# Twelve-layer decoder on one core: the second attention's rotation and its clears go from GpSimd to VectorE

## The chip, the cores and the metric

The kernel runs on one core of one Trainium2 chip. The core has TensorE for matrix products (PE, with its weight loads PEld shown apart), VectorE (DVE), ScalarE (ACT), GpSimd (POOL) and SyncE (SP), which issues the transfers. The metric is the device time of one execution in microseconds (us), lower is better. A profiled execution gives, besides its own time, a trace of every instruction. TensorE's clock is granted by the chip and is seen in the trace as a share of full speed: 1.00, or 0.50.

## The reference

A post-norm decoder of four levels with three sublayers each, on x of shape 4 x 256 x 256 (1024 rows, handled as 8 tiles of 128) and a context of 4 x 256 x 128:

```python
x = layernorm(x + L0_attn(x));  x = layernorm(x + L0_ssm(ctx, x));  x = layernorm(x + L0_ffn(x))
x = layernorm(x + L1_attn(x));  x = layernorm(x + L1_ssm(ctx, x));  x = layernorm(x + L1_ffn(x))
...
```

The second attention, L1, is what is changed. It has 16 query heads and 4 key heads of 16 columns, and a rotation of neighbouring column pairs before the scores:

```python
x0, x1 = xp[..., 0], xp[..., 1]
r0 = x0 * cos - x1 * sin
r1 = x0 * sin + x1 * cos
...
weights = softmax(Qr @ Kr.T / 4);  out = (weights @ V) @ W_o
```

The L1 state-space layer (`ssm`) depends on the context alone until its last gate, so the kernel runs its scan beside other layers. The L0 feed-forward layer, here called the thought layer, makes four small refinement steps on the last row of each batch and gates the result into all rows.

## The kernel before

`decoder` runs the parts of a list one after the other (first attention, thought, second attention, experts and so on); x (128 rows x 8 tiles x 256) and its transpose xT stay in SBUF. The order in which each engine's instructions stand is fixed when the program is built: a planner merges what the code emits, so an instruction can stand well ahead of its place in the code once its memory is free. Each engine then works through its own queue in order and waits at an instruction until its inputs are there.

Three helpers matter: `K.tt` is a tensor-tensor operation on VectorE (profile line L111), `K.ptt` the same on GpSimd (L123), `K.mm` a product on TensorE (L132). `K.copy` alternates between VectorE (L98) and ScalarE (L100). `norm` (L153) takes the moments on VectorE (L160, L161), makes rstd in two GpSimd instructions (`root`: L169 and a power, L123) and scales x on VectorE (L117); then `turn_pair` (L182) transposes x on TensorE (L187).

The second attention is `run_gqa` (L982). It takes five tiles and clears parts of them: `kn` (keys as rows, L994 and L995), `qn` (queries as rows, L996), and `vt` (values, L997 and L998), besides `ones` (L999 to L1001). The head slots are 32 columns wide, and 16 of them are padding that must be zero, or one in the keys' maximum column. These clears stand on GpSimd between the end of the first attention and the start of the thought layer, at 378 to 384 us.

Then, for each of the 8 tiles: the products with the query, key and value weights go to one PSUM bank (`ps`, three banks), VectorE makes four products with cosine and sine into t0 to t3 (L1016 to L1019), the differences and sums of these go into `qn` (16 heads) and `kn` (4 heads) (L1020 to L1022), two copies put the values into `vt`, and the transposes of the tile before follow (`small_heads_T`, L787). Between the tiles stand the first steps of the row maxima (`heads16.begin`: score products `sc`, and reduces on VectorE, L129) and, per tile, one step of the scan (`K.scans.beside(1)`): two exponentials on ScalarE, and on VectorE a product with B, the scan (L520) and a product with C, later summed on TensorE into `ssmps`. After the eight tiles `heads16.run` goes on with scores, exponentials and sums, one scan step to each.

In the thought layer the names that the prediction uses are `w_d` (the weights whose mean is taken out), `centre`, `mean` and `cb` (set up on VectorE, L637 to L671), the gates of the 8 tiles (`gate`, L679, then one sigmoid), `xb` and `gx` (on GpSimd), and the scan's preparation: taps on the context, `u`, `xd`, `delta`, `du` (L451 to L487).

Of the kernel before, what the change touches and what calls it, by code (L numbers as in the profile page):

```python
# [29 lines left out]
ADD, SUB, MUL, MAX, MIN = ALU.add, ALU.subtract, ALU.mult, ALU.max, ALU.min  # L30
# [503 lines left out]
def gate_pair(K, pool, y, b):  # L534

    K.scans.upto(b)
    gate = pool.tile([P, DC, L], F32, name="gate")

    K.act(gate, K.x[:, 2 * b : 2 * b + 2, :], AF.Silu)
    K.ptt(gate, gate, y[:, :, b * L : (b + 1) * L], MUL)  # L540
    for t in range(2):
        ps = K.tp.tile([P, 512], F32, name="ps", tag="tp")
        for c in range(DC):
            K.nc.tensor.transpose(ps[:, c * P : (c + 1) * P], gate[:, c, t * P : (t + 1) * P], K.ident)
        K.add_out(2 * b + t, ps[:, 0:D])
# [236 lines left out]
def small_heads_T(K, dst, src, col, chunks, scales=None, tp=None):  # L782


    ps = (tp or K.tp).tile([P, 4, P], F32, name="ps", tag="tp")
    for c in range(chunks):
        K.nc.tensor.transpose(ps[:, c, :], src[:, c * P : (c + 1) * P], K.ident)  # L787
    if scales is None:
        K.copy(dst[:, :, col : col + P], ps[:, 0:chunks, :])
    else:  # L790
        for lo, hi, g, b in scales:
            K.copy_scaled(dst[:, :, col + lo : col + hi], ps[:, 0:chunks, lo:hi], g, b)
# [189 lines left out]
def run_gqa(K, w, more):  # L982
    nc, tc = K.nc, K.tc
    more()
    with ExitStack() as ctx:
        one = ctx.enter_context(tc.tile_pool(name="gqa1", bufs=1))
        wk = ctx.enter_context(tc.tile_pool(name="gqa2", bufs=2))
        qT = one.tile([P, 4, B * L], F32, name="qT")
        kT = one.tile([P, 1, B * L], F32, name="kT")
        qn = one.tile([P, NT, 16, 32], F32, name="qn")  # L990
        kn = one.tile([P, NT, 4, 32], F32, name="kn")
        vt = one.tile([P, NT, 4, 2, 32], F32, name="vt")
        ones = one.tile([P, 2, 32], F32, name="ones")
        nc.gpsimd.memset(kn[:, :, :, 16:32], 0.0)  # L994
        nc.gpsimd.memset(kn[:, :, :, 16:17], 1.0)  # L995
        nc.gpsimd.memset(qn[:, :, :, 16:32], 0.0)  # L996
        nc.gpsimd.memset(vt[:, :, :, 0, 16:32], 0.0)  # L997
        nc.gpsimd.memset(vt[:, :, :, 1, 0:16], 0.0)  # L998
        nc.gpsimd.memset(ones, 0.0)  # L999
        for j in range(2):  # L1000
            nc.gpsimd.memset(ones[:, j, 16 * j : 16 * j + 16], 1.0)  # L1001
        ctx.enter_context(K.turns(1))
        if K.first == 3 and K.fused(3):
            K.scans.begin("l1x")
        heads16 = SmallHeads(K, ctx, "gqa", qn, qT, kT, vt, ones, w["o"], [(0, L)])
        early = ctx.enter_context(ExitStack())
        pm = early.enter_context(tc.tile_pool(name="gqap", bufs=3, space=PSUM))
        for i in range(NT):
            ps = pm.tile([P, 512], F32, name="ps")
            for c in range(DC):  # L1010
                K.mm(ps[:, 0:384], K.xT[:, c, i * P : (i + 1) * P], w["qkv"][:, c, :], c == 0, c == DC - 1)
            pair = ps[:, 0:320].rearrange("p (h j two) -> p h j two", j=8, two=2)
            x0, x1 = pair[:, :, :, 0], pair[:, :, :, 1]
            cos, sin = (w["rope"][:, k, i % 2, :].rearrange("p (h j) -> p h j", j=8) for k in range(2))
            t = [wk.tile([P, 20, 8], F32, name=f"t{k}") for k in range(4)]
            K.tt(t[0], x0, cos, MUL)  # L1016
            K.tt(t[1], x1, sin, MUL)
            K.tt(t[2], x0, sin, MUL)
            K.tt(t[3], x1, cos, MUL)  # L1019
            for dst, hs in ((qn, slice(0, 16)), (kn, slice(16, 20))):  # L1020
                K.ptt(dst[:, i, :, 0:8], t[0][:, hs], t[1][:, hs], SUB)
                K.ptt(dst[:, i, :, 8:16], t[2][:, hs], t[3][:, hs], ADD)  # L1022
            for j in range(2):
                K.copy(vt[:, i, :, j, 16 * j : 16 * j + 16], ps[:, 320:384].rearrange("p (h d) -> p h d", d=16))
            for k in ([i - 1] if i else []) + ([i] if i == NT - 1 else []):
                small_heads_T(K, qT, qn[:, k].rearrange("p h s -> p (h s)"), k * P, 4)
                small_heads_T(K, kT, kn[:, k].rearrange("p h s -> p (h s)"), k * P, 1)

            heads16.begin((0, 0, 1, 1, 1, 1, 2, 2)[i])
            K.scans.beside(1)  # L1030
        early.close()
        if K.fused(3):
            heads16.then = lambda b: gate_pair(K, wk, K.scans.y, b)
        heads16.run(ctx, lambda: K.scans.beside(1))
# [1183 lines left out]
def load_none(K, wp):  # L2218
# [5 lines left out]
    (load_none, run_gate("l0x")),  # L2224
    (load_thought, run_thought),
    (load_gqa, run_gqa),
    (load_none, run_gate("l1x")),
    (load_moe, run_moe),
# [209 lines left out]
```

## Time and profile before

| what | us |
|---|---|
| median of three runs (lowest, highest) | 2461.45 (2458.55, 2464.18) |
| the profiled execution | 2461.66 |
| its span on the engines | 2459.9 |
| mean granted TensorE clock | 0.947 |
| busy: TensorE, VectorE, ScalarE, GpSimd | 2267.6, 1464.3, 801.9, 288.5 |
| the clears of the second attention, on GpSimd | 378.7 to 384.1 |
| the thought layer, about | 374 to 526 |
| the rotation of the second attention, first to last product with the weights | 527.7 to 562.0 |
| rest of the second attention and of the scan, about | 562 to 756 |

The span starts with the first instruction and ends with the last; the execution is some 1.8 us longer than it. Busy time of a stage is no measure of what it costs: an engine that is filled may still be waited for by nobody. What a change is worth is read where the wait ends last: a line of the view in time shows an instruction's start and duration, and in brackets how long its engine stood idle before it and whose result ended the wait.

### The profile page before, as it was taken

How to read it: one execution, taken by the hardware profiler on the slowest of the kernel's cores; microseconds unless marked ns; L12 is line 12 of the kernel's file. 1: busy time of each engine (PE TensorE's matmuls, PEld its weight loads, DVE VectorE, ACT ScalarE, POOL GpSimd, SP SyncE). 2: the span in 40 equal slices, each digit the busy share in tenths (PEclk: the TensorE clock that was granted, in tenths of full speed). 3: DMA queues.
4: the chain of work that ended last, by engine and by line, in shares of the span. 5: the costliest groups of instructions: out<-in, count | busy, mean ns of one | idle time of the engine just before them, and what ended most of it. 6: DMA issues, size and time to landing. Idle time of an engine off the chain costs nothing. (4 is left out here: it accounts for less than half of the span.)

```text
span 2459.9 us, 28697 instructions
## 1 busy us (share of the span) xinstructions
PE 2267.6 (92%) x10620; PEld 1520.1 (62%) x10624; DVE 1464.3 (60%) x2986; ACT 801.9 (33%) x1781; POOL 288.5 (12%) x455
## 2 busy tenths in 40 slices
PE   8899997769996999899999999999999988899997
PEld 4566763335433555536888888888776543476774
DVE  4799982888985211280455544445556677774566
ACT  3577664513441111162211111111022244343434
POOL 0000014130010322200011000110210002100001
PEclk9999997767887999999999999999998899999999
DMA  6222221312213544220222112110100002100000
GB/s 201 61 60 60 53 61 27 80 41 48 52 39 101 164 131 127 81 78 9 73 82 87 46 46 73 47 63 31 46 22 1 20 18 71 41 1 1 1 1 18
DMA packets 132835, 138.99 MB, mean 57 GB/s; under 512 B 13876, under 2 KB 120726, under 8 KB 130904
## 3 DMA queue, kind: packets, MB, share of 16 engines
q1 hardware_dynamic: 132696, 137.16, 19.5%
q8 instruction: 84, 1.38, 0.2%
q14 instruction: 55, 0.45, 0.1%
HBM read 134.27 MB, written 2.85 MB: 56 GB/s over the span
## 5 line engine op out<-in xcount | busy, mean ns | idle before, releaser
L132 PE MATMUL ps<-xw,xcT 128*128 128x256 f32 (+1 forms) x2304 | 518.9, 382 | 0.3 <-ACT YT L126 0.3
L132 PEld LDWEIGHTS ps<-xw,xcT 128*128 128x128 f32 x2304 | 430.8, 190 | 64.0 <-issue 1.9
L132 PE MATMUL sc<-kT,qT 32*128 32x256 f32 (+2 forms) x1024 | 239.2, 404 | 9.6 <-DVE qn L129 9.2
L132 PEld LDWEIGHTS sc<-kT,qT 128*128 128x128 f32 (+1 forms) x1024 | 152.6, 200 | 86.0 <-issue 52.4
L111 DVE TENSOR_TENSOR xp<-ps,xb 128x256 f32<-128x256 f32 x96 | 40.4, 421 | 230.7 <-PE ps L132 230.6
L126 ACT ACTIVATE dA<-delta,negA 128x255 f32<-128x255 f32 x256 | 118.2, 501 | 142.0 <-DVE s L520 139.1
L132 PE MATMUL ssmps<-s,idz 128*128 128x512 f32 x256 | 146.7, 678 | 18.9 <-DVE s L111 18.0
L520 DVE TENSOR_TENSOR_SCAN s<-dA,s 128x512 f32<-128x512 f32 x128 | 155.0, 1218 | 2.6
L126 ACT ACTIVATE p<-sc,nm 128x256 f32<-128x256 f32 (+1 forms) x256 | 112.0, 444 | 96.5 <-DVE nm L129 90.5
L111 DVE TENSOR_TENSOR hT<-u,a 128x512 f32<-128x512 f32 x48 | 33.1, 690 | 184.0 <-PE u L132 184.0
L126 ACT ACTIVATE sq<-xp 128x1024 f32<-128x1024 f32 x24 | 25.4, 1057 | 314.1 <-DVE xp L111 314.1
L132 PE MATMUL o<-pT,vt 128*128 128x256 f32 (+1 forms) x352 | 116.2, 452 | 12.3 <-ACT pT L332 11.9
L169 POOL TENSOR_SCALAR rstd<-mv 128x2 f32<-128x2 f32 x48 | 11.8, 245 | 887.5 <-DVE mv L161 877.7
L129 DVE TENSOR_REDUCE qn<-sc 128x2 f32<-128x480 f32 (+1 forms) x192 | 87.0, 505 | 37.9 <-PE sc L132 36.4
L126 ACT ACTIVATE e<-sT 128x512 f32<-128x512 f32 x128 | 70.9, 591 | 108.4 <-PE sT L132 108.2
L132 PE MATMUL sT<-q,kT 32*128 32x256 f32 (+1 forms) x384 | 102.3, 508 | 3.5 <-ACT e L126 3.3
L1474 DVE TENSOR_TENSOR_SCAN dec<-xT,idz 128x256 f32<-128x256 f32 (+1 forms) x192 | 89.7, 535 | 21.5 <-DMA xT<-ad 21.5
L129 DVE TENSOR_REDUCE nm<-sc 128x2 f32<-128x512 f32 (+1 forms) x128 | 77.3, 612 | 41.2 <-PE sc L132 40.7
L126 ACT ACTIVATE a<-g 128x512 f32<-128x512 f32 x48 | 28.7, 598 | 206.2 <-PE g L132 203.4
L111 DVE TENSOR_TENSOR s<-du,bc 128x512 f32<-128x512 f32 x128 | 87.7, 691 | 11.0 <-POOL du L123 7.7
L123 POOL TENSOR_TENSOR xp<-xp,rn 128x128 f32<-128x128 f32 x96 | 35.2, 403 | 476.9 <-DVE rn L1406 476.9
L132 PE MATMUL g<-xT,wj 128*128 128x512 f32 x192 | 90.3, 593 | 0.7 <-ACT rows L100 0.7
(503 smaller groups left out, 4027.2 us busy)
## 6 DMA issues: line engine op xcount, KB each, us to landing
bc<-bcd SPq DMA_DIRECT2D x128, 256.0 KB, 4.6
xw<-in_l2a_xw_dram SPq DMA_DIRECT2D x24, 768.0 KB, 4.8
xT<-ad SPq DMA_DIRECT2D x12, 1024.0 KB, 4.3
wj<-in_l1f_gate_dram SPq DMA_DIRECT2D x48, 128.0 KB, 2.7
wj<-in_l1f_up_dram SPq DMA_DIRECT2D x48, 128.0 KB, 2.9
wj<-in_l1f_down_dram SPq DMA_DIRECT2D x48, 128.0 KB, 3.1
sel<-cwd SPq DMA_DIRECT2D x32, 192.0 KB, 3.2
sel<-cwd SPq DMA_DIRECT2D x32, 128.0 KB, 3.5
```

The lines of the kernel that those rows point to most:

```text
L111: self.nc.vector.tensor_tensor(out=out, in0=a, in1=b, op=op)
L123: self.nc.gpsimd.tensor_tensor(out=out, in0=a, in1=b, op=op)
L126: self.nc.scalar.activation(out, in_, func, **kw)
L129: self.nc.vector.tensor_reduce(out=out, in_=in_, axis=AX.X, op=op, **kw)
L132: self.nc.tensor.matmul(out, lhsT=lhsT, rhs=rhs, start=start, stop=stop)
L169: self.nc.gpsimd.tensor_scalar(out=out, in0=in_, scalar1=add, scalar2=None, op0=ADD)
L520: nc.vector.tensor_tensor_scan(out=s.rearrange("p c l -> p (c l)"), data0=dA.rearrange("p c l -> p (c l)"), data1=s.rearrange("p c l -> p ...
L1474: nc.vector.tensor_tensor_scan(out=dec[:, k, h, :], data0=ap[:, h, at(bb, k, j) : at(bb, k, 2)], data1=K.idz[:, 0 : (2 - j) * P], initial=0.0,
```

## The change

The five clears of `kn`, `qn` and `vt` are issued on VectorE; the clears of `ones` stay on GpSimd. In the rotation the four differences and sums of each tile are issued on VectorE; for the eight tiles these are 32 instructions.

```diff
-        nc.gpsimd.memset(kn[:, :, :, 16:32], 0.0)
-        nc.gpsimd.memset(kn[:, :, :, 16:17], 1.0)
-        nc.gpsimd.memset(qn[:, :, :, 16:32], 0.0)
-        nc.gpsimd.memset(vt[:, :, :, 0, 16:32], 0.0)
-        nc.gpsimd.memset(vt[:, :, :, 1, 0:16], 0.0)
+        nc.vector.memset(kn[:, :, :, 16:32], 0.0)
+        nc.vector.memset(kn[:, :, :, 16:17], 1.0)
+        nc.vector.memset(qn[:, :, :, 16:32], 0.0)
+        nc.vector.memset(vt[:, :, :, 0, 16:32], 0.0)
+        nc.vector.memset(vt[:, :, :, 1, 0:16], 0.0)
         nc.gpsimd.memset(ones, 0.0)
...
             for dst, hs in ((qn, slice(0, 16)), (kn, slice(16, 20))):
-                K.ptt(dst[:, i, :, 0:8], t[0][:, hs], t[1][:, hs], SUB)
-                K.ptt(dst[:, i, :, 8:16], t[2][:, hs], t[3][:, hs], ADD)
+                K.tt(dst[:, i, :, 0:8], t[0][:, hs], t[1][:, hs], SUB)
+                K.tt(dst[:, i, :, 8:16], t[2][:, hs], t[3][:, hs], ADD)
```

With the change the planner places the clears on VectorE behind x, the weight column, `centre` and `mean` of the thought layer's set-up, around `cb` and the first gate eviction. The new differences and sums stand directly behind the four products of their tile; in one tile two row maxima stand between them. Transfers are issued in the same order as before. Some instructions near both places change their order on TensorE and ScalarE: a sigmoid and an absolute value of the scan's preparation, and a few score products and products with the weights in the rotation.

## The prediction

> **What bounds the kernel now.** Part 1 of the page first, for the whole span:
>
> ```profile
> PE 2267.6 (92%) x10620; PEld 1520.1 (62%) x10624; DVE 1464.3 (60%) x2986; ACT 801.9 (33%) x1781; POOL 288.5 (12%) x455
> ```
>
> TensorE is the long engine and GpSimd the idle one, but that is an average over twelve layers. The chain of what ended last cannot help here: its list of pieces reaches back to 1780 us only, and the change acts at 378 to 384 us (the clears) and 530 to 570 us (the rotation). So I read those two places in the view in order of time, and the stretches around them in the table by stretches.
>
> The clears, in order of time, one engine after the other (start, duration, engine, line, what, and in brackets the idle time before it):
>
> ```profile
> 375.97 2.81 POOL L123 TENSOR_TENSOR xb<-x,r_l0f_rows 128x256 f32<-128x256 f32 x4
> 378.73 0.51 POOL L994 MEMSET kn<- 128x512 f32 x1
> 379.19 1.79 POOL L996 MEMSET qn<- 128x2048 f32 x1
> 380.97 0.21 POOL L169 TENSOR_SCALAR rstd<-mv 128x2 f32<-128x2 f32 x1
> 381.12 0.14 POOL L995 MEMSET kn<- 128x32 f32 x1
> 381.19 0.51 POOL L997 MEMSET vt<- 128x512 f32 x1
> 381.67 0.70 POOL L123 TENSOR_TENSOR rstd<-rstd,power 128x2 f32<-128x2 f32 x1
> ...
> 382.41 1.00 DVE L117 TENSOR_SCALAR x<-x,mv,rstd 128x256 f32<-128x256 f32 x2 [4.28 <-POOL rstd L123]
> ...
> 383.24 1.13 PE L187 MATMUL ps<-idz,x 128*128 128x128 f32 x4 [4.22 <-DVE x L117]
> ```
>
> The reader is to see a queue on GpSimd that costs time: the variance was ready at 377.18, the two instructions that make rstd of it stand behind and between four clears, VectorE waits 4.28 us for rstd and TensorE 4.22 us for VectorE. Nothing else runs on TensorE then.
>
> The stretches (busy us with counts for PE, PEld, DVE, ACT, POOL; then the granted clock, the DMA share, GB/s):
>
> ```profile
> 379.00:383.00 4.00, 0.01 (x1) 0.00 (x0) 0.59 (x1) 0.00 (x0) 3.94 (x8) 0.78 0.00 0
> 383.00:392.00 9.00, 8.76 (x26) 5.05 (x27) 1.34 (x5) 5.66 (x12) 1.61 (x4) 0.53 0.00 0
> 530.00:545.00 15.00, 14.23 (x61) 8.10 (x60) 13.26 (x34) 3.83 (x13) 6.52 (x16) 0.95 0.20 50
> 545.00:552.00 7.00, 7.00 (x13) 3.46 (x13) 4.15 (x12) 0.40 (x2) 1.28 (x4) 0.51 0.15 37
> 552.00:569.00 17.00, 16.02 (x71) 8.57 (x70) 15.30 (x32) 4.55 (x13) 4.97 (x12) 1.00 0.15 32
> 569.00:600.00 31.00, 31.00 (x116) 17.42 (x117) 25.83 (x39) 9.84 (x20) 0.16 (x1) 0.51 0.22 49
> 600.00:645.00 45.00, 43.51 (x318) 21.41 (x318) 40.71 (x59) 19.91 (x41) 0.93 (x2) 1.00 0.30 58
> ```
>
> In the rotation two limits alternate. At full clock VectorE is filled (13.26 of 15 us, 15.30 of 17), and TensorE follows it. At half clock (545 to 552, 569 to 600) TensorE is filled and VectorE waits. GpSimd limits nothing there. Its two groups in 527 to 580 us, and where TensorE last waited before the long slow stretch:
>
> ```profile
> L123 POOL TENSOR_TENSOR qn<-t,t 128x128 f32<-128x128 f32 x16 | 9.8, 611 | 30.9 <-DVE t L111 30.9
> L123 POOL TENSOR_TENSOR kn<-t,t 128x32 f32<-128x32 f32 x16 | 4.0, 250 | 0.0
> ...
> 568.01 1.16 PE L132 MATMUL ssmps<-s,idz 128*128 128x512 f32 x2 [0.84 <-DVE s L111]
> ```
>
> GpSimd waits 30.9 us for VectorE. In the other direction the waits in 527 to 580 us hold 1.8 us of weight loads waiting for its qn and kn, in three waits.
>
> **The clears, taken off GpSimd.** Five clears go (514, 1794, 142, 514, 514 ns). In the built order GpSimd now has, behind the four xb, the three clears of `ones` (rows 0.14 and 0.15 for two) and then the two of rstd. The xb end at 378.78; 0.2 for the small clears puts the first at 379.0. The second starts 0.44 later where nothing stands between them (519.73 to 520.17 in the thought's end), takes 0.70 and ends at 380.1. VectorE's x starts 0.04 behind it (382.37 to 382.41), so at 380.15 for 382.41: 2.3 us sooner, and the transposes on TensorE with it (0.83 behind x, as now). Bounds: 2.2 to 2.4.
>
> **The clears, put on VectorE.** In the built order they stand behind x, the weight column, `centre` and `mean`; ScalarE waits for `mean` (7.62 us now), so that must not get late: 380.15 + 1.00 + 0.45 + 0.24 + 0.79 = 382.6, for 384.12 now. The trace has no clear on VectorE. From above: its reduce over the same 2048 elements takes 2.25 us. From below: GpSimd's own rows, 1.79. The Trainium skill (VectorE: DVE Perf Modes, Zero memsets can be issued as uint32) says a clear takes one cycle per element; at that page's 0.96 GHz 2048 elements are an estimated 2.13 us. I take 2.2, 0.6 for each of the three of 512 and 0.15: 4.2 us (3.5 to 4.5). They lie in VectorE's idle time, 2.98 us before `cb` (L671) and 6.47 us before the first gate eviction at 393.79. Queued behind them are `cb`, not read before `cs` at 417.8, and the gate evictions, which TensorE feeds later than the clears end. Cost nothing; without that cover up to 4.2.
>
> Sum of this place: -2.3 us. It is carried on, because TensorE has no gap from 383.24 to 404 and everything behind (conv taps, u, xd, delta) is released by it. The new order also sets one absolute value behind the sigmoid on ScalarE, and the token's turn ahead of the second x_proj product on TensorE; each moves a step by a microsecond or two, in both directions, and I set that at 0, bounds -1 to +1.5.
>
> **The rotation, put on VectorE.** Per tile of 128 rows two instructions of 128 elements and two of 32, eight tiles. The nearest VectorE rows are its four products of 160 elements: 312 ns each, but the four take 1.01 together, so a pitch of 0.235, that is 0.167 for the elements and 0.07 fixed. That makes 0.20 for 128 elements and 0.10 for 32; the sum that reads t3 straight behind its product waits for it another 0.1. Per tile 2 x 0.20 + 2 x 0.10 + 0.1 = 0.7, for eight 5.6 us (0.6 and 4.8 without that wait; 0.9 and 7 if every duration counts in full). Off GpSimd go 13.8 us that nobody but the transposes waited for.
>
> How much of 5.6 reaches the end? Behind the new instructions in VectorE's queue stand the vt copy, the eviction of qT, the scan step and the row maxima, and TensorE waits for these: the score banks are freed by the maxima. From 534.1 to 548.8 VectorE is busy without a gap, and tiles 0 to 4 fall before its end: tile 0 costs 0.5 (it waited 0.53 for TensorE behind it), 1 to 3 cost 0.7 each before TensorE's release at 545. But the tail behind tile 4 is hidden in the 2.85 us that VectorE waits for TensorE at 551.66. There tile 5 is 1.9 late. Tile 5 adds 0.7, and what tile 6 adds goes into the wait of 1.34 before the eviction at 563.43, whose chain on TensorE starts before it: 2.6 late. Tile 7 adds 0.7. So 3.3 us arrive at 570, and from there TensorE at half clock carries it unshortened. Bounds: 1.5 (the later qn no longer wait for GpSimd's 1.6 us per tile) to 5.6.
>
> A shared port is removed, too: one GpSimd qn took 1371 ns, against a median of 457, beside a scan of 1.31 for 1.22. Worth 0.1 to 0.3 on VectorE; inside the bounds.
>
> **The clock.** The trace: TensorE's clock halved at 381.6, 2.6 us after its last product; but also at 545.4 and 569.0, where it had just waited 0.47 and 0.84 us, with 0.6 and 0.9 us of idle time in the three us before. The Trainium skill (TensorE: Matmul & The Clock Gate, HAM oscillation) asks only that no gap pass some 3.4 us. By that rule added VectorE work, which makes gaps of 0.7 us, costs no clock, and the sum is -2.3 + 3.3 = +1.0. By this case's rows gaps of that size are what starts a slow stretch, so the rule does not hold here, and the measurement decides. TensorE will now wait up to 0.7 us more per tile where it waits on VectorE. The short slow stretch, 545.4 to 551.5, holds 6.1 us that are 3.05 us at full clock. I charge one more of these in 552 to 569, and that the long one starts with the score products at 566.03 and not at 569.0, 3 us at half clock, of which 1.5 are lost: together 4.5. Bounds: 0, and 8.5 if all of 552 to 569 runs at half clock.
>
> **Sum.** -2.3 + 3.3 + 4.5 = +5.5 us. The profiled execution took 2461.66 (span 2459.9 and 1.8 around it) and would take 2467.2; that execution is 0.2 above the median of 2461.45, so the median goes to 2467.0. 0.2%, 4.9 us, is about what a measurement of this kernel can tell from no change (its three runs span 0.23%).
>
> **Rivals.**
> *The work moves, the clock doesn't.* Slow stretches as now: +1.0, 2462.5 (-1.5 to +4). For it: the first drop follows TensorE's own waits for ScalarE, not VectorE. Against: 552 to 569 is at full clock with only 1 us of TensorE idle.
>
> *Faster, by the clock at the clears.* TensorE's gap at 379 shrinks from 4.2 to 1.9 us, below the 2.6 after which the clock fell. If it then stays up, 383.2 to 391.6 loses half of its 8.4 us: -4.2 more, -6.5 with the 2.3. This decides if the rotation then costs under 1.6 us, which it does if the later tiles' transposes come early enough to feed the slow stretch, or that stretch of 31 us ends sooner: VectorE has 5.2 us idle in it, all there is to win. With 0.5 for the rotation: -6.0, 2455.5. For it: the gap is arithmetic from rows. Against: gaps under a microsecond also brought the clock down.
>
> *Hidden anyway.* Rotation and clears both cost and bring nothing. The 4.22 us that TensorE waited for the clears speak against it; it lands at 2461.5 and is counted with the first rival.
>
> **How the numbers follow.** Forecast 0.42 (0.36 slower by over 0.2%, 0.06 within; its own range 2464 to 2475). First rival with "hidden" 0.28 (0.25 within, 0.03 slower). Clock at the clears 0.30 (0.24 faster, 0.05 within, 0.01 slower). That makes faster 0.24, within 0.36, slower 0.40. The range takes in the forecast up to +15 (5.6 arriving and 8.5 of clock, with 1.5 of order) and the faster case down to -8: 2453 to 2476.
>
> **What would show it.** x (L117) at about 380.2 and TensorE's gap there near 1.9 us; the granted clock of 383 to 392 above 0.9 would speak for the faster rival. Clears on VectorE of 2.1 to 2.3 us for qn. Thirty-two small products on VectorE, 0.7 us a tile. The end of the rotation about 1 us later against the start of the thought layer's gates if the clock stays; a stretch at 0.5 within 552 to 569 if I am right. I am wrong if the last rotation tile comes no later behind the first than now (37.4 us).

## The result: slower, and not where the sum put it

The changed kernel takes 2474.61 us (median of five runs, 2470.99 to 2478.76) against 2462.17 us of the kernel before (2458.55 to 2473.50, five runs); the ratio is 1.0044 [1.0027, 1.0061], that is 6.6 to 15 us more. The forecast of 2467.0 named the right sign, and the time lies in its range, but the two terms that made the sign, the rotation and the clock, are not what costs.

The profiled execution took 2478.76 us, the slowest of the five, with a span of 2477.0. It arrives at the clears 1.8 us later than the profiled execution before (first `xb` at 376.08 for 374.28), although nothing ahead of them differs. So stages are compared below by their own lengths, and totals by medians.

First the whole span, part 1 of the page of the changed kernel:

```profile
PE 2272.5 (92%) x10624; PEld 1525.6 (62%) x10624; DVE 1483.1 (60%) x3023; ACT 801.7 (32%) x1781; POOL 271.7 (11%) x418
```

VectorE's busy time rose by 18.8 us and GpSimd's fell by 16.8. The rotation's sums (6.2 busy, shown below) and the clears (3.3) explain 9.5 of VectorE's 18.8; the other 9.3 are more than covered by one waiting instruction, which counts as busy and is 10.6 us longer than before.

The clears, in order of time, in the changed kernel:

```profile
380.51 0.17 POOL L999 MEMSET ones<- 128x64 f32 x1
380.73 0.16 POOL L1001 MEMSET ones<- 128x16 f32 x2
380.86 0.22 POOL L169 TENSOR_SCALAR rstd<-mv 128x2 f32<-128x2 f32 x1
381.16 0.71 POOL L123 TENSOR_TENSOR rstd<-rstd,power 128x2 f32<-128x2 f32 x1
381.90 0.74 DVE L117 TENSOR_SCALAR x<-x,mv,rstd 128x256 f32<-128x256 f32 x2 [2.34 <-POOL rstd L123]
...
382.46 0.78 PE L187 MATMUL ps<-idz,x 128*128 128x128 f32 x4 [1.64 <-DVE x L117]
384.06 0.48 DVE L994 MEMSET kn<- 128x512 f32 x1
384.68 2.05 PE L132 MATMUL ps<-w_l0f_gate,xT 128*128 128x256 f32 x4
384.92 1.76 DVE L996 MEMSET qn<- 128x2048 f32 x1 [0.37 <-issue]
387.17 0.09 DVE L995 MEMSET kn<- 128x32 f32 x1
387.29 0.48 DVE L997 MEMSET vt<- 128x512 f32 x1
387.83 0.48 DVE L998 MEMSET vt<- 128x512 f32 x1
```

This place does what was forecast. VectorE waits 2.34 us for rstd instead of 4.28, TensorE 1.64 for 4.22. The clears take 3.3 us on VectorE and end at 388.3. One gate eviction stands among them (386.77); the next comes only when TensorE feeds it (391.75), and TensorE waits for none of this.

Now the place where the time goes. This is the token's turn in the thought layer of the changed kernel, in order of time:

```profile
401.08 1.91 ACT L126 ACTIVATE gate<-gate 128x2048 f32<-128x2048 f32 x1
401.17 0.38 PE L684 MATMUL last<-idz,xT 128*4 128x128 f32 x2
402.90 0.67 ACT L126 ACTIVATE du<-ssmps,w_l1x_cols 128x512 f32<-128x512 f32 x1
403.08 0.22 POOL L169 TENSOR_SCALAR trstd<-tmv 4x1 f32<-4x1 f32 x1 [19.10 <-DVE tmv L604]
403.38 0.56 POOL L123 TENSOR_TENSOR trstd<-trstd,power 4x1 f32<-4x1 f32 x1
403.92 1.39 POOL L123 TENSOR_TENSOR gx<-gate,r_l0f_rows 128x256 f32<-128x256 f32 x2
403.98 11.00 DVE L117 TENSOR_SCALAR r<-tok,tmv,trstd 4x256 f32<-4x256 f32 x1 [0.99 <-POOL trstd L123]
...
413.44 1.39 POOL L123 TENSOR_TENSOR gx<-gx,x 128x256 f32<-128x256 f32 x2
415.02 0.86 DVE L111 TENSOR_TENSOR r<-r,r_l0f_rows 4x256 f32<-4x256 f32 x2
415.93 0.37 PE L612 MATMUL ps<-idz,r 4*128 4x4 f32 x2 [14.39 <-DVE r L111]
416.24 3.64 PE L132 MATMUL ssmps<-u,w_l1x_xp 128*40 128x512 f32 x4
419.80 1.87 PE L132 MATMUL ps<-rT,w_l0f_agg 128*128 128x4 f32 x8
```

And the same steps in the kernel before:

```profile
406.78 0.40 DVE L117 TENSOR_SCALAR r<-tok,tmv,trstd 4x256 f32<-4x256 f32 x1 [0.99 <-POOL trstd L123]
407.21 0.86 DVE L111 TENSOR_TENSOR r<-r,r_l0f_rows 4x256 f32<-4x256 f32 x2
408.51 1.41 POOL L123 TENSOR_TENSOR gx<-gate,r_l0f_rows 128x256 f32<-128x256 f32 x2 [1.77 <-ACT gate L126]
```

One VectorE instruction on 4 x 256 elements, the scaling of the token, takes 11.00 us instead of 0.40. It starts 0.06 us after GpSimd has begun its sixteen `gx` instructions, and ends 0.15 us after the last of them. TensorE stands still for 14.39 us behind it. Before, `gx` waited for the sigmoid (1.77 us) and came only when `r` was done. In the changed kernel the sigmoid stands ahead of the second absolute value on ScalarE (401.08, then 402.90), so the gates are ready before the token is, and `gx` starts first.

The gap costs more than its length. Behind it TensorE ran at half clock: the granted clock of 415 to 424 us was 0.50. In the kernel with the clears alone (below), which has the same order and the same gap here, it was 0.71 in 413 to 420, and from `last` to the first square it took 20.6 us for 22.7.

Last the rotation of the changed kernel, in the table by stretches (the columns as in the prediction), from the first products with the weights on:

```profile
536.00:552.00 16.00, 15.05 (x53) 8.73 (x54) 14.79 (x46) 4.27 (x12) 0.00 (x0) 0.83 0.14 37
552.00:564.00 12.00, 11.76 (x51) 6.70 (x50) 12.00 (x30) 2.77 (x8) 0.00 (x0) 1.00 0.20 41
564.00:572.00 8.00, 5.90 (x21) 2.51 (x19) 8.00 (x24) 1.74 (x6) 0.00 (x0) 0.81 0.26 49
572.00:582.00 10.00, 9.83 (x29) 5.48 (x30) 8.43 (x20) 1.82 (x5) 0.00 (x0) 0.50 0.14 32
582.00:612.00 30.00, 30.00 (x125) 16.51 (x123) 24.03 (x35) 10.08 (x21) 0.00 (x0) 0.59 0.22 50
612.00:657.00 45.00, 43.09 (x317) 21.32 (x315) 42.24 (x61) 21.29 (x42) 1.95 (x3) 1.00 0.27 57
```

VectorE is filled (12.00 of 12 us, 8.00 of 8), as forecast. But no slow stretch was added: the stretch at full clock reaches from 552 to about 568, and the long slow one follows it for some 40 us (0.50, then 0.59), where before a short one (545 to 552) and a long one (569 to 600) stood. Over 75 us that begin some 9 us behind the first product with the weights the mean granted clock is the same, 0.75 (537 to 612 us before, 547 to 622 changed), and TensorE is busy for 72.96 and 72.49 us of them. The sums of the rotation on VectorE, among the groups of 537 to 590 us:

```profile
L111 DVE TENSOR_TENSOR qn<-t,t 128x128 f32<-128x128 f32 x16 | 3.9, 286 | 0.0
L111 DVE TENSOR_TENSOR kn<-t,t 128x32 f32<-128x32 f32 x16 | 2.3, 188 | 0.0
```

From the first pair of `qn` (542.05) to that of `kn` (542.45) and the copy behind it (542.66) it is 0.61 us a tile, 4.9 for eight; 5.6 was the estimate. From the first of these sums to the last of the eight tiles it is 37.6 us, before 37.4.

### The profile page after: what moved, and what is told of

It is laid out like the page before. It is cut to its first block, busy times and chain, and to the rows that moved or that the text cites. A ratio compares the mean times of both kernels' runs of the same rounds, so it can differ in the third digit from the quotient of the medians.

```text
span 2477.0 us, 28684 instructions
## 1 busy us (share of the span) xinstructions
PE 2272.5 (92%) x10624; PEld 1525.6 (62%) x10624; DVE 1483.1 (60%) x3023; ACT 801.7 (32%) x1781; POOL 271.7 (11%) x418
## 5 line engine op out<-in xcount | busy, mean ns | idle before, releaser
L132 PEld LDWEIGHTS ps<-xw,xcT 128*128 128x128 f32 x2304 | 430.8, 190 | 64.0 <-issue 1.9
L132 PE MATMUL sc<-kT,qT 32*128 32x256 f32 (+2 forms) x1024 | 242.1, 408 | 10.0 <-DVE qn L129 9.7
L132 PE MATMUL ssmps<-s,idz 128*128 128x512 f32 x256 | 145.9, 676 | 19.6 <-DVE s L111 18.8
L132 PE MATMUL u<-xT,wj 128*128 128x512 f32 x192 | 90.9, 595 | 0.0
```

Source lines behind the costliest of these rows:

```text
L132: self.nc.tensor.matmul(out, lhsT=lhsT, rhs=rhs, start=start, stop=stop)
```

## The experiments

The two theories. A: the loss comes from one collision. A VectorE instruction that needs an access to SBUF which, by this theory, it shares with GpSimd is held up while GpSimd's `gx` run back to back, and only the order brought about by the early clears lets the two meet. B is the prediction's: the clears gain, the added VectorE work in the rotation and the clock lose.

To compare profiles I measured each stage in the trace, in us, between marks that all kernels have: the first `xb` (376.08 above), the transposes into `last` (L684 above), the first square of the refinement steps (`sq`), the copy `lastmean` at their end, the first product with the weights of the second attention, its last `kn`, and the first copy of the experts' gates (`cwT`). Kernels that leave work out are not in the table.

| kernel | xb to last | to sq | to lastmean | to weights | to last kn | to cwT | sum |
|---|---|---|---|---|---|---|---|
| before | 29.9 | 6.9 | 67.8 | 48.8 | 41.2 | 242.9 | 437.5 |
| changed | 25.1 | 22.7 | 65.4 | 48.8 | 41.6 | 243.8 | 447.4 |
| clears alone | 25.1 | 20.6 | 64.9 | 48.8 | 40.7 | 242.5 | 442.7 |
| rotation alone | 29.0 | 6.9 | 67.0 | 48.8 | 41.7 | 242.4 | 435.9 |
| changed, token in PSUM | 25.1 | 8.5 | 66.8 | 48.8 | 42.3 | 242.2 | 433.7 |
| changed, scaling reads PSUM | 23.4 | 21.9 | 63.0 | 48.8 | 41.6 | 243.8 | 442.5 |
| changed, gx behind th | 25.1 | 10.1 | 68.0 | 48.8 | 42.5 | 244.4 | 439.0 |
| changed, token and th from PSUM | 26.7 | 12.4 | 63.3 | 48.8 | 41.6 | 243.7 | 436.5 |
| before, token in PSUM | 29.9 | 7.1 | 67.7 | 48.8 | 41.1 | 243.0 | 437.5 |
| changed, gx in pairs of tiles | 26.8 | 21.6 | 65.3 | 48.8 | 42.2 | 242.1 | 446.8 |
| changed, gx in halves | 25.1 | 12.6 | 68.4 | 48.8 | 41.7 | 243.9 | 440.5 |
| clears alone, token and th from PSUM | 23.4 | 8.1 | 67.0 | 48.8 | 40.9 | 242.7 | 430.8 |

The row of the kernel before and its control (fourth from below) differ by 0.2 us at most in any stage. Kernels with the same order still differ with the clock: the first column is 23.4, 25.1 and 26.7 us in three kernels with the clears on VectorE (scaling reads PSUM, changed, token and `th` from PSUM), at a mean granted clock of 1.00, 0.93 and 0.87. And behind the experts, where all kernels have the same code, the profiled executions took between 1648 and 1664 us. So a row says where time went in one execution; whether a kernel is faster is read from the medians.

### Each half of the change alone

The clears alone (the rotation stays on GpSimd, the clears as in the changed kernel):

```diff
-                K.tt(dst[:, i, :, 0:8], t[0][:, hs], t[1][:, hs], SUB)
-                K.tt(dst[:, i, :, 8:16], t[2][:, hs], t[3][:, hs], ADD)
+                K.ptt(dst[:, i, :, 0:8], t[0][:, hs], t[1][:, hs], SUB)
+                K.ptt(dst[:, i, :, 8:16], t[2][:, hs], t[3][:, hs], ADD)
```

> The five clears on VectorE, the rotation left on GpSimd. In the thought layer this kernel has the order of the changed kernel on every engine. Theory A (the port): there the sigmoid now stands ahead of the second absolute value, so GpSimd's 16 gx instructions start just before VectorE scales the last token's row (r, 4x256), and that instruction, 0.40 us before, lasts as long as they do, 11 us; expected r at 10 to 11 us and 2469 to 2473, nearly the whole loss. Theory B (the prediction's: VectorE's load in the rotation and the clock): the clears alone gain 2.3, 2459.

Measured: 2471.48 us (2468.63 to 2483.07), ratio to the kernel before 1.0037 [1.0021, 1.0054]. The scaling lasts 11.006 us, from 402.10, with `gx` from 402.05.

The rotation alone (the clears go back to GpSimd, the rotation stays on VectorE):

```diff
-        nc.vector.memset(kn[:, :, :, 16:32], 0.0)
...
+        nc.gpsimd.memset(kn[:, :, :, 16:32], 0.0)
```

> The rotation's differences and sums on VectorE, the clears left on GpSimd; the thought layer's order is that of the kernel before. Theory A: r stays at 0.40 us, and the rotation costs between nothing and 3 us: 2460 to 2465. Theory B: 3.3 of VectorE's time and 4.5 of clock, 2469.

Measured: 2464.41 us (2459.62 to 2470.35), ratio 0.9997 [0.9982, 1.0012]. The scaling takes 0.40 us. The stage from the weights to the last `kn` has 41.7 us for 41.2.

So nearly the whole loss comes with the clears, and the rotation costs nothing that these times can tell: the interval of -0.18 to +0.12% is -4.4 to +3 us, and B's 3.3 + 4.5 = 7.8 lies outside it. B falls. What this pair does not tell is whether the 11 us are the cause, for the clears also change the order in the thought layer.

### The collision taken apart by what VectorE reads

The token's scaling and its two products work in place on the PSUM tile `last`, so that none of them reads SBUF twice:

```diff
-            K.ts(r, t[:, 0, :], mv[:, 0, 0:1], rstd, SUB, MUL)
+            K.ts(last, last, mv[:, 0, 0:1], rstd, SUB, MUL)
...
-        K.tt(r, r, row["in_g"][0:B, :], MUL)
-        K.tt(r, r, row["in_b"][0:B, :], ADD)
+        K.tt(last, last, row["in_g"][0:B, :], MUL)
+        K.tt(r, last, row["in_b"][0:B, :], ADD)
```

> The changed kernel, with the last token's row scaled, multiplied and summed out of PSUM (each of the three instructions with at most one SBUF input and a PSUM operand), nothing else. Theory A: they last 0.4 us each beside gx, the layer gets back 10 us and keeps the 2.3 of the clears: 2460 to 2464. Theory B: no change against the changed kernel, 2472 to 2475.

Measured: 2463.37 us (2459.49 to 2478.39), ratio 1.0002 [0.9989, 1.0014]. VectorE in order of time, with `gx` running from 401.60 to 412.55:

```profile
401.66 0.54 DVE L117 TENSOR_SCALAR last<-last,tmv,trstd 4x256 f32<-4x256 f32 x1 [0.99 <-POOL trstd L123]
402.23 0.42 DVE L111 TENSOR_TENSOR last<-last,r_l0f_rows 4x256 f32<-4x256 f32 x1
402.68 0.41 DVE L111 TENSOR_TENSOR r<-last,r_l0f_rows 4x256 f32<-4x256 f32 x1
...
407.32 5.26 DVE L120 SCALAR_TENSOR_TENSOR th<-w_l0f_cols,th 128x8 f32<-128x8 f32 x1 [0.73 <-PE ps L132]
412.50 0.15 DVE L115 TENSOR_SCALAR rstd<-ps 128x4 f32<-128x4 f32 x1
```

The scaling ran in the middle of `gx` in 0.54 us. The block came back at the next instruction with two inputs in SBUF, the sum `th` on eight columns (0.17 us in the changed kernel), which ended with `gx`. TensorE waited 3.01 us for it. The loss is gone from the time all the same; why `th` costs so little is seen in the last kernel of this section.

In the next kernel only the scaling reads PSUM; its result and the products stay in SBUF:

```diff
-            K.ts(r, t[:, 0, :], mv[:, 0, 0:1], rstd, SUB, MUL)
+            K.ts(r, last, mv[:, 0, 0:1], rstd, SUB, MUL)
```

> As the run before, but only the scaling reads PSUM; its product with the gain row still reads two SBUF tensors. Theory A1 (only an instruction that takes both of VectorE's ports to one tensor is held up): 2460 to 2464. Theory A2 (one with two SBUF inputs is held up too): the product waits in the scaling's place, some 10 us, 2470 to 2474. Theory B: 2472 to 2475.

Measured: 2471.95 us (2466.37 to 2486.11), ratio 1.0041 [1.0020, 1.0063]. VectorE in order of time:

```profile
398.21 0.53 DVE L117 TENSOR_SCALAR r<-last,tmv,trstd 4x256 f32<-4x256 f32 x1 [0.99 <-POOL trstd L123]
398.78 11.02 DVE L111 TENSOR_TENSOR r<-r,r_l0f_rows 4x256 f32<-4x256 f32 x2
```

The block moved on by one instruction: of the two products, which read SBUF twice, one lasts 10.57 us and the other 0.41. Both kinds are held up, a scaling with its only tensor in SBUF and a product with two. What reads PSUM and one SBUF input is not.

The two kernels differ in what VectorE reads, but the first of them also has another order on TensorE (the x_proj product ahead of the token's transposes), so they don't give the price of the collision alone.

### The collision alone, in the same order

One GpSimd copy of eight elements, later overwritten, makes `gx` wait for `th`:

```diff
         gx = one.tile([P, NT, D], F32, name="gx")
+        nc.gpsimd.tensor_copy(gx[:, :, 0], th.rearrange("p c b -> p (c b)"))
```

> The changed kernel with one GpSimd copy of 8 elements from th into gx ahead of gx's products, which makes all of gx wait for the token's chain; the copied values are overwritten. TensorE, VectorE and ScalarE keep the changed kernel's order in every instruction. Theory A: the scaling falls to 0.4 us, the token's steps run alone, gx comes after them and meets no VectorE operation that reads SBUF twice; 10 us or so come back and the gain at the clears stays: 2459 to 2465. Theory B (the rotation and the clock make the loss): 2470 to 2476, as the changed kernel. If the cost of the changed order (an absolute value behind the sigmoid) lies anywhere else than in this collision, it also stays at 2470 or above.

Measured: 2467.89 us (2462.79 to 2481.57, 22 runs), ratio 1.0021 [1.0007, 1.0036]. In order of time:

```profile
403.40 0.40 DVE L117 TENSOR_SCALAR r<-tok,tmv,trstd 4x256 f32<-4x256 f32 x1 [0.99 <-POOL trstd L123]
...
405.06 3.27 PE L132 MATMUL ssmps<-u,w_l1x_xp 128*40 128x512 f32 x4
408.26 1.05 PE L132 MATMUL ps<-rT,w_l0f_agg 128*128 128x4 f32 x8
...
418.59 1.02 PE L132 MATMUL ps<-w_l0f_d,tT 128*4 128x256 f32 x2 [3.75 <-DVE tT L111]
```

TensorE, VectorE and ScalarE have the changed kernel's order, instruction by instruction; on GpSimd one instruction came forward (the first power of the steps, into the run of `gx`). From `last` to the first square it takes 10.1 us for 22.7, and to the weights of the second attention (the first four columns of the table) 152.1 for 162.0. So the collision by itself is worth 10 us there. In the medians 6.7 us come back (2474.61 to 2467.89), less than the 10 to 15 that I had expected; by the ratios, each to the kernel before measured beside it, 0.23% or 5.7 us. The two intervals overlap, so the times alone don't show that this kernel is faster than the changed one; the 10 us stand in the two traces. The rest of the way explains part: the stages to `kn` and `cwT` are 1.5 us longer than in the changed kernel. And the refinement steps take 2.6 us longer (68.0 for 65.4), since the power now stands among the `gx` and TensorE waits 3.75 us for what hangs on it.

The same rows show a second cost of the order. From `last` to `sq` it is 10.1 us without any collision, against 6.9 before: the x_proj product (3.27 us) now stands between the token's transposes and the products that need them.

### How long VectorE is held

`gx` on half of the columns, with the sums that read it likewise (the kernel leaves out the other half):

```diff
-            K.ptt(gx[:, i, :], gate[:, i, :], row["bc_b"], MUL)
-            K.ptt(gx[:, i, :], gx[:, i, :], K.x[:, i, :], ADD)
+            K.ptt(gx[:, i, 0:P], gate[:, i, 0:P], row["bc_b"][:, 0:P], MUL)
+            K.ptt(gx[:, i, 0:P], gx[:, i, 0:P], K.x[:, i, 0:P], ADD)
```

> The changed kernel with gx made for columns 0 to 127 of each tile only (16 GpSimd instructions of 128x128 instead of 128x256, and the sums that use gx likewise); the other half of gx is left out, so the output is that of another layer. Up to gx no engine's order changes. If VectorE's scaling of the token lasts as long as GpSimd's unbroken run of gx (theory A), it shrinks with that run: 16 instructions at about 0.40 us (the row of another GpSimd product of 128 columns) are 6.4 us, so the scaling takes 6 to 7 us for 11.0. If it is held for a fixed time, or for one instruction of GpSimd, it stays at 11.0 or falls to some 0.8 us. By theory B nothing is said of it.

Measured: the scaling takes 0.53 us, the products 0.63 and 0.56, and three of the `gx` beside them are lengthened (0.49, 0.69 and 0.63 us for 0.44). The expectation of 6 to 7 us missed: here the two engines took turns. A single run took 2462.64 us.

Three more kernels asked whether the size of the GpSimd instructions decides. `gx` of four tiles only, at full width (tiles 4 to 7 then use the `gx` of tiles 0 to 3, so it computes something else):

```diff
         for i in range(NT):
-            K.ptt(gx[:, i, :], gate[:, i, :], row["bc_b"], MUL)
-            K.ptt(gx[:, i, :], gx[:, i, :], K.x[:, i, :], ADD)
+            if i < 4:
+                K.ptt(gx[:, i, :], gate[:, i, :], row["bc_b"], MUL)
+                K.ptt(gx[:, i, :], gx[:, i, :], K.x[:, i, :], ADD)
```

> The changed kernel with gx made for tiles 0 to 3 only: 8 GpSimd instructions of 128x256 back to back for 16 (tiles 4 to 7 then add the gx of tiles 0 to 3, so the output is that of another layer). The run with half of the columns showed 0.53 us for the scaling, so not every back-to-back run of GpSimd holds VectorE up. If instructions of this size hold it for as long as they follow each other, the scaling now lasts the length of the shorter run: 8 times 0.68 us, 5.4 to 5.6 us. If the collision needs a long run, or if the half-column kernel escaped by chance, 0.5 or 11 us.

Measured: 5.567 us for the scaling; the run of eight `gx` ended 5.48 us after its start. A single run took 2474.15 us.

`gx` of two tiles in one instruction:

```diff
+        for i in range(0, NT, 2):
+            ii = slice(i, i + 2)
+            K.ptt(gx[:, ii, :], gate[:, ii, :], row["bc_b"].unsqueeze(1).to_broadcast([P, 2, D]), MUL)
+            K.ptt(gx[:, ii, :], gx[:, ii, :], K.x[:, ii, :], ADD)
         for i in range(NT):
-            K.ptt(gx[:, i, :], gate[:, i, :], row["bc_b"], MUL)
-            K.ptt(gx[:, i, :], gx[:, i, :], K.x[:, i, :], ADD)
```

> The changed kernel with gx made for two tiles in one instruction: 8 GpSimd instructions of 128x512. From 0.41 us apart at 128 columns and 0.68 at 256, 512 should stand 1.2 us apart. If what matters is that the instruction is long (128 columns let VectorE in, 256 do not), the scaling lasts until the end of the run, some 9.7 us. If 256 columns are a coincidence of periods, it is let in after one instruction: 1.3 to 1.7 us.

Measured: 9.881 us; the eight `gx` stand 1.22 us apart and end 9.79 us after their start. A single run took 2474.45 us.

`gx` in two halves of its columns, nothing left out:

```diff
         for i in range(NT):
-            K.ptt(gx[:, i, :], gate[:, i, :], row["bc_b"], MUL)
-            K.ptt(gx[:, i, :], gx[:, i, :], K.x[:, i, :], ADD)
+            for h in (slice(0, P), slice(P, D)):
+                K.ptt(gx[:, i, h], gate[:, i, h], row["bc_b"][:, h], MUL)
+                K.ptt(gx[:, i, h], gx[:, i, h], K.x[:, i, h], ADD)
```

> The changed kernel with gx made in two halves of its columns: 32 GpSimd instructions of 128 columns, nothing left out. If the size of the GpSimd instruction decides, the scaling is let in as in the half-column run, 0.5 to 0.6 us, although GpSimd's run is as long as ever (32 times 0.41 is 13 us); the kernel then takes 2461 to 2468. If the length of the run decides, the scaling lasts 13 us and the kernel 2473 to 2479.

Measured: 2473.25 us (2464.40 to 2482.37, 15 runs), ratio 1.0030 [1.0017, 1.0044]. In order of time:

```profile
403.85 0.53 DVE L117 TENSOR_SCALAR r<-tok,tmv,trstd 4x256 f32<-4x256 f32 x1 [0.99 <-POOL trstd L123]
404.42 1.22 DVE L111 TENSOR_TENSOR r<-r,r_l0f_rows 4x256 f32<-4x256 f32 x2
...
413.60 3.93 DVE L120 SCALAR_TENSOR_TENSOR th<-w_l0f_cols,th 128x8 f32<-128x8 f32 x1 [1.96 <-PE ps L132]
```

The scaling is let in as forecast, but the forecast time (2461 to 2468) is missed. `th`, later in the same run of small `gx`, is held for 3.93 us, until the last of them ends, and the steps take 3.0 us longer than in the changed kernel (68.4 for 65.4). That is not enough: up to the experts its trace is still 6.9 us ahead of the changed kernel (440.5 for 447.4), while its median is 1.4 below, with overlapping intervals. Its profiled execution was the slowest of the 15, with the 1664 us behind the experts; where the rest of its loss lies is open. As to the hold, a GpSimd instruction of 128 columns can hold VectorE up like one of 256, and the size alone does not decide. Nor does a full-width `gx` always lock VectorE out: in the kernel before, `th` meets them too and takes 0.23 us, in the control below 0.76. Held to the end of the run were the scaling at 16, at 8 and at 8 double `gx`, a product, and two of the `th`. What decides between being let in at the next change of GpSimd instructions and waiting through all of them is open; the only thing the held cases share is that they end 0.03 to 0.28 us after the end of the run (the product last, at 409.35 for 409.07).

### A version without the collision, and its control

The token's steps in place in PSUM as in the third run, and `th` from the PSUM result of its product with a column made beforehand (`last` is then summed from `th2`):

```diff
+        ab = one.tile([P, DC], F32, name="ab")
+        K.stt(ab, d2b, 4.0, w["cols"][:, 0, :], MUL, ADD)
...
-        K.stt(th, wide(d2b, B), 4.0, th, MUL, ADD)
+        th2 = one.tile([P, DC, B], F32, name="th2")
+        K.tt(th2, ps, wide(ab, B), ADD)
```

> The changed kernel with the token normed in place in PSUM (as in the third run), and the later sum th made from the PSUM result of the product and a column computed beforehand, so that no VectorE operation beside gx reads SBUF twice. Theory A: scaling, products and both th take under 0.6 us each; the 5.26 us that th lost in the third run come back: 2456 to 2462, a little below the kernel before. If another cause holds the stage, 2463 or above.

Measured: 2463.86 us (2453.38 to 2475.01, 14 runs), ratio 0.9997 [0.9977, 1.0018]. Every step of the token beside `gx` takes 0.54 us or less. By its median it is no better than the version with `th` held up, and the hope of a few us below the kernel before was not fulfilled. Its trace can't be set against that version's stage by stage: from `last` to the first square it took 12.4 us at a granted clock of 0.56 (399 to 411), where the last kernel below, with the same edits, took 8.1 at 0.95.

The control, the kernel before with the token's steps in PSUM (the first diff of this group on the kernel before):

> Control: the kernel before with the token normed in place in PSUM. Before, the token's scaling ran at 0.4 us with gx coming later, so theory A expects no gain from it: 2460 to 2466, ratio within 0.2% of 1. If it is clearly faster, the PSUM form brings something of its own, and the third run's gain must not be laid to the collision alone.

Measured: 2464.74 us (2456.27 to 2478.29, 14 runs), ratio 0.9999 [0.9979, 1.0020]. The PSUM form brings nothing of its own.

And the clears alone with both PSUM edits:

> The clears on VectorE, the rotation left on GpSimd, and the token's steps without two reads of SBUF (as in the run with th from PSUM). Theory A: the clears alone cost 8.7 us only by the collision (2471.5), so without it they bring the gain at the start of the thought layer: 2458 to 2464, 8 to 12 us below the clears alone. Theory B says nothing against it, but if the clears' loss lies elsewhere it stays near 2471.

Measured: 2460.25 us (2454.28 to 2478.49, 22 runs), ratio 0.9996 [0.9980, 1.0013], against 1.0037 [1.0021, 1.0054] for the clears alone. In its trace it is 6.7 us ahead of the kernel before at the experts (430.8 for 437.5), and 11.9 ahead of the clears alone; but this execution was the fastest of the 22 (2454.28), and its clock stayed up at the clears. The intervals of the two kernels with the clears don't meet. So what these edits change is shown to carry the loss: the collision, and with it the place of the x_proj product, which runs ahead of the token's transposes here, too, and which the kernel with `gx` behind `th` put at 3.2 us. That this version beats the kernel before is not shown.

The same trace shows why `th` costs so little. The variance of the first refinement step is ready for GpSimd at 405.50, but its power stands behind all of `gx` in GpSimd's queue:

```profile
407.86 1.39 POOL L123 TENSOR_TENSOR gx<-gx,x 128x256 f32<-128x256 f32 x2
409.21 1.02 POOL L123 TENSOR_TENSOR rstd<-rstd,power 128x4 f32<-128x4 f32 x1
410.27 0.17 DVE L111 TENSOR_TENSOR tT<-ps,rstd 128x8 f32<-128x8 f32 x1 [4.76 <-POOL rstd L123]
410.49 1.01 PE L132 MATMUL ps<-w_l0f_d,tT 128*4 128x256 f32 x2 [4.13 <-DVE tT L111]
```

The step cannot go on before `gx` ends, whether `th` is held until then or not.

## Why the prediction was right in sign and wrong in cause

**The clears off GpSimd: right, and somewhat too low.** x was to start 2.3 us sooner, and so it did, counted from the first `xb` (5.8 us for 8.1); VectorE's wait shrank by 1.9 and TensorE's gap by 2.6. The stage from `xb` to `last` shrank by more, from 29.9 to 25.1, because the slow stretch behind the gap is milder, too: the granted clock was 0.93 and 0.70 in 382 to 385 and 385 to 390, for 0.54 and 0.50 in 381 to 384 and 384 to 389 before. In the clears-alone kernel with the PSUM edits it stayed at 1.00 throughout and the stage took 23.4. Here the rival "faster, by the clock at the clears" (-6.5) had it right, in part (0.81 over the 383 to 392 us for which I had named 0.9 as its sign) or, in that other execution, in full; I had given it 0.30.

**The clears on VectorE: right.** 3.3 us for an estimated 4.2, in idle time. The 2048 elements took 1.76 us, below the bound of 1.79 from GpSimd's own row; the rule weighed there (the Trainium skill, VectorE: DVE Perf Modes, Zero memsets can be issued as uint32) made it 2.13, too high for this form.

**The order, set at 0: this is the step that failed.** "The new order also sets one absolute value behind the sigmoid on ScalarE, and the token's turn ahead of the second x_proj product on TensorE; each moves a step by a microsecond or two, in both directions, and I set that at 0, bounds -1 to +1.5." I asked what each moved instruction delays, and not what the earlier sigmoid releases: `gx`, eleven microseconds of GpSimd without a pause, 0.06 us ahead of an instruction that shares an access with it. Measured in the trace of the kernel with the same order and no collision, the term is 3.2 us for the order on TensorE (10.1 for 6.9) and 10 for the collision at the second attention, the half clock behind the gap included: 13 where at most 1.5 stood.

The rule for it was in the prediction's reach. The Trainium skill (SBUF — State Buffer, Who interferes with whom) says that a VectorE instruction in a 2-port mode and a GpSimd instruction lock each other out, that one with two SBUF inputs contends with a GpSimd instruction that reads SBUF, and that one with at most one SBUF input outside those modes does not. I used the shared port only for what the rotation gains. The runs agree with the rule in kind: the product with two SBUF inputs was held (10.57 us), the forms with PSUM ran beside `gx` in 0.54 and 0.42. The scaling, held for 11.00 us, has only one tensor as input; that it runs in a 2-port mode no run here shows. They don't agree in size. By the page the first to come holds the pair for its whole instruction: one `gx`, 0.71 us. Measured is a wait over sixteen of them, 11.00 us. With the page's size the edit would have cost at most 0.7 us for each of the token's three steps, 2 us in all, and the forecast would hardly have moved.

**The rotation: over-estimated.** Its 0.61 us a tile is near the 0.7 of the working: the sums start 0.20 and 0.10 us apart, as estimated, and the extra wait of 0.1 did not come. But of 5.6 us I let 3.3 arrive, at least 1.5. From the weights to the last `kn` the four kernels with the rotation on GpSimd take 40.7 to 41.2 us and those with it on VectorE 41.6 to 42.5: about 1.0 arrives. The sign of being wrong that the prediction names, a last tile no later behind the first than 37.4 us, was missed by 0.2 (37.6); it says little, for kernels with the same rotation on VectorE have 37.6 to 38.5, those with it on GpSimd 36.9 to 37.4.

**The clock: wrong.** The 4.5 us charged for slow stretches did not come. The short stretch vanished and the long one came earlier. From the last `kn` to the experts it takes 242.5 to 243.0 us with the rotation on GpSimd and 242.1 to 244.4 with it on VectorE. That small gaps stood ahead of two slow stretches was read rightly from the rows. That more small gaps make more slow time was only an estimate, and is not so; nor is a gap needed. In the changed kernel the second part of the long stretch began at 586 us: the clock was 0.93 in 582 to 586 and 0.50 in 586 to 610, and TensorE was busy throughout as far as the profile shows (4.00 of 4 us, 24.00 of 24).

**The sum.** At the weights of the second attention the changed kernel is 8.6 us longer: -4.8 (to `last`), +15.8 (to `sq`), -2.4 (to `lastmean`). To the experts another 1.3 come, 9.9 in all, within the 6.6 to 15 us of the medians. The predicted +5.5 has the right sign only because 3.3 + 4.5, which did not come, stood in for an order and a collision that it had at 0. That the time fell into the range is luck as well: the upper end adds 5.6, 8.5 and 1.5 and leaves out the -2.3 of the clears; with it the sum is 13.3, 2474.8, and the measured 2474.61 lies just inside, for other reasons. Of the rivals, "hidden anyway" was right of the rotation, and the faster one of the clears; the case that decided stood in no rival.

## What to carry to other kernels

When a change moves an instruction forward in one queue, ask also what it releases sooner, and what that meets: a long back-to-back run on GpSimd can be a hazard for any VectorE instruction that reads SBUF twice, or scales from SBUF to SBUF, however small it is. A look for one tiny VectorE operation at twenty times its usual duration finds such a place at once in the view by time; giving that operation its input in PSUM, or making GpSimd's run wait for it, removed it here; the second put 2.6 us on the steps behind. And part the change in two before explaining it by its largest part: here the part that looked dear cost nothing that could be measured, and the part that looked like a gain carried the loss.

## What was not expected of the hardware

VectorE can be shut out for a whole run of GpSimd instructions, not only for one: 11.0 us over sixteen, 5.57 over eight, 9.88 over eight twice as long, 3.93 over the rest of 32 half as long. In other cases it is let in at once or behind one instruction (0.23, 0.53, 0.76 us), under conditions that these runs don't settle. While it waits, the profile counts it as busy: the 11 us stand in VectorE's busy time and not in a wait, and the view of waits names only the engines behind it (TensorE's 14.39 us for `r`).

The long stretch at half clock in the second attention began 31, 41 and 31 us behind the first product with the weights in three kernels (rotation alone, before, changed) with nearly the same work, lasted some 30 to 40 us each time (in two of them with a short break) and left the length of the stages behind it unchanged within 2 us. What starts and ends it is not settled here.
